# Routing of the third batch spread over more slots of the attention, and the experts' tile tables made in four pieces

## The chip, the core and the metric

The kernel runs on one core of a Trainium2 chip. Five engines work beside each other, each in the order of its own program: TensorE (PE in the profile; its weight loads are PEld), VectorE (DVE), ScalarE (ACT), GpSimd (POOL), and SyncE (SP), which issues most of the DMAs. They meet at semaphores. The metric is the time of one execution on the device in microseconds (us). The median of three runs before the change is 1767.79 us (1761.07 to 1770.71).

## The reference

Four blocks follow each other, each on the sum of what came before it and its own input normalised. x has the shape (4, 512, 256), that is 4 batches of 512 tokens. All is float32.

```python
x = x + linear_attention(layernorm(x))       # layer 0
x = x + hadamard_ffn(layernorm(x))
x = x + grouped_attention(layernorm(x))      # layer 1
x = x + attention_and_experts(layernorm(x))  # the block that is changed
```

The last block, with 32 query heads, 8 key heads, 16 experts and 4 experts to a token:

```python
h = rms(x, ln_w)
q, k = rope(h @ wq, h @ wk); v = h @ wv
scores = where(causal, q @ k.T / 8, -1e30)
x = x + (softmax(scores) @ v) @ wo
h = rms(x, ff_ln_w)
logits = h @ wg                              # (token, 16)
topv, topi = top_k(logits, 4)
weights = zeros.at[topi].set(softmax(topv))
a = silu(h @ w1[e]) * (h @ w3[e])            # for every expert e
moe = sum over e of weights[:, e] * (a @ w2[e])
out = x + moe
```

The kernel computes each token for its four experts alone.

## The kernel before

**Attention.** Each batch has four pairs of key heads, so there are 16 pairs, u = 0 to 15 (NU). A pair's scores are made in five fills f = 0 to 4, and one loop counts them as n = 5u + f, from 0 to 79, with four more turns, 80 to 83, in which only what is left of pair 15 is done. A turn does, in this order on each engine's program:

- fill (line 1287): PE makes the scores sc, in four PSUM banks.
- weighed (1408): DVE multiplies the products po of the pair before with the inverse sums (rsb) into oT; turn_blocks (1333): DVE transposes the last fill's exps into pT.
- inverses (1398): PE transposes the widened inverse sums into pq; out_proj (1421): PE multiplies oT with wo into py; q_lo and q_hi (1209, 1215): PE makes the next queries (pr), for ACT to copy (raw) and POOL to rotate (qr).
- least (1306): DVE masks the scores and takes their minima mx, which frees the banks sc.
- A string of signs for ACT (line 1888): a digit is the exps of one bank (exps, 1323), a "w" the widening of an inverse sum (widen, 1391), and a "." one copy out of PSUM that was put off (drain_one), if there is one.
- weigh (1354): PE makes the products po of exps and values, in parts: "3" at the end of fill 4 of the same pair (224 matmuls in the records), "02" in fill 0 and "1" in fill 1 of the next pair (168 and 104).

Everything on PE but the scores shares four further PSUM banks in turn (unit, line 1120). po takes all four. The copy y of py is added to z by POOL (line 1434).

**Routing.** When a batch's attention is done, each token's experts are chosen. route (line 1439) returns this work as a list of pieces: squares, mean, root, scale, rows_out, residual, turn_half, turned_both, logits, ranks (two, each with earlier and count), gates, shares, places, choose, and 16 scatters. A scatter is an indirect DMA of POOL that writes 128 tokens' rows to their place in the table xs in DRAM. Pieces are plain (False), use a PSUM bank (True), are scatters (None), or a pause, behind which only scatters follow in that slot. extras (line 1770) takes as many pieces as it is told. Every turn ends in a slot: extras with 1 to 3 plain pieces, up to 1 with a bank (only in fills 2 and 3) and 2 or 4 scatters (line 1901). In fill 1 of the odd pairs there is another slot in the middle, for one piece with a bank (line 1883).

Batch 2's routing (the third batch) is put in the list in fill 64, and its pieces run to the end of turn 82. Behind its choose comes plan_tiles(0).

**The tables of tiles.** The experts work in 79 tiles of 128 rows (NSLOT). A tile's expert, its first row and its row count come from the counts of rows by expert. plan_tiles (line 1662) makes a table of them in some 40 small DVE instructions; SP writes it to DRAM (list) and reads it back for all partitions (tall, lines 1746 and 1748). read_plan (1753) turns it into integers. There are two tables: phase 0, after batch 2, lays out 33 tiles (NFIRST), which hold rows of the first three batches only; phase 1, after batch 3, lays out the other 46.

**Experts.** Behind the attention a loop of steps n works on the tiles (lines 2037 to 2056): fetch_weights loads an expert's weights into wall, which takes the space of the attention's buffers; fetch_rows loads a tile's rows (xin), three steps ahead; turn_in transposes them (ptx, hTx); hidden makes ph, gx and ax; turn_hidden transposes (pa, aTx); give multiplies (pyx), weighs (yx) and adds to the result by an indirect DMA of POOL. Each step ends with two pieces of batch 3's routing, the list `pieces` (1918): 34 of them in steps 0 to 16, then plan_tiles(1), five empty ones, and read_plan(1).

Of the kernel before, what the change touches and what calls it, by code (L numbers as in the profile page):

```python
# [16 lines left out]
P = 128  # L17
# [9 lines left out]
NEXP = 16  # L27
# [62 lines left out]
def kernel(  # L90
# [64 lines left out]
    def C(name):  # L155
        cols = C_COLS[name]
        if cols.start < C_L0:
            return c_l0[0][:, cols]
        return cst[:, cols.start - C_L0 : cols.stop - C_L0]
# [782 lines left out]
    with ExitStack() as a1:  # L942
# [109 lines left out]
        for k in range(4 * NT * B + 2):  # L1052
            b, i = divmod(k, 4 * NT)
# [55 lines left out]
    with ExitStack() as a2:  # L1109
# [28 lines left out]
        def drain_one():  # L1138
            if held:
                held.pop(0)()  # L1140
# [521 lines left out]
        def plan_tiles(phase):  # L1662

            lo, hi = PHASES[phase]
            pos = C("iota")

            def small(name, n=NEXP):
                return rp.tile([P, n], F32, tag=name, name=name)

            cnt, tiles, first = small("cnt"), small("tiles"), small("first")  # L1670
            nc.vector.tensor_scalar(cnt, C("e16"), -float(CAP), 1.0, ALU.mult, ALU.add)
            nc.vector.tensor_tensor(cnt, cnt, run, ALU.add)

            cube = rp.tile([P, NEXP, NEXP], F32, tag="cube", name="cube")
            wide = [P, NEXP, NEXP]
            some = cnt
            if phase == 0:
                some = small("some")
                nc.vector.tensor_scalar(some, cnt, 0.5 - P, None, ALU.add)
            nc.vector.tensor_tensor(  # L1680
                cube, some.unsqueeze(2).to_broadcast(wide),
                C("m128").unsqueeze(1).to_broadcast(wide), ALU.is_gt,
            )
            nc.vector.tensor_reduce(tiles, cube, AX.X, ALU.add)
            nc.vector.tensor_tensor(tiles, tiles, taken, ALU.subtract)
            nc.vector.tensor_tensor(
                cube, C("before").rearrange("p (e f) -> p e f", f=NEXP),
                tiles.unsqueeze(1).to_broadcast(wide), ALU.mult,
            )
            nc.vector.tensor_reduce(first, cube, AX.X, ALU.add)  # L1690
            mine, past = small("mine"), small("past")
            nc.vector.tensor_scalar(mine, first, pos, None, ALU.is_le)
            nc.vector.tensor_tensor(past, first, tiles, ALU.add)
            nc.vector.tensor_scalar(past, past, pos, None, ALU.is_gt)
            nc.vector.tensor_tensor(mine, mine, past, ALU.mult)


            if phase == 0:


                nc.vector.tensor_scalar(
                    taken, first, -1.0, float(hi - lo), ALU.mult, ALU.add
                )
                nc.vector.tensor_scalar(taken, taken, 0.0, None, ALU.max)
                nc.vector.tensor_tensor(taken, taken, tiles, ALU.min)
                used, ahead, all_ = small("used"), small("ahead"), small("all", 1)
                nc.vector.tensor_scalar(used, taken, 0.0, None, ALU.is_gt)
                nc.vector.tensor_reduce(all_, used, AX.X, ALU.add)
                nc.vector.tensor_tensor(
                    cube, C("before").rearrange("p (e f) -> p e f", f=NEXP),  # L1710
                    used.unsqueeze(1).to_broadcast(wide), ALU.mult,
                )
                nc.vector.tensor_reduce(ahead, cube, AX.X, ALU.add)

                nc.vector.tensor_tensor(place, C("e16"), ahead, ALU.subtract)
                nc.vector.tensor_scalar(place, place, all_, None, ALU.add)
                nc.vector.tensor_tensor(ahead, ahead, place, ALU.subtract)
                nc.vector.tensor_tensor(ahead, ahead, used, ALU.mult)
                nc.vector.tensor_tensor(place, place, ahead, ALU.add)
            info = rp.tile([P, 5, NEXP], F32, tag="info", name="info")  # L1720
            off = small("off")
            if phase == 0:
                nc.vector.tensor_scalar(off, first, -1.0, None, ALU.mult)
            else:
                nc.vector.tensor_tensor(off, taken, first, ALU.subtract)
            nc.vector.tensor_scalar(off, off, float(P), None, ALU.mult)
            nc.vector.tensor_copy(info[:, 0, :], C("e16"))
            nc.vector.tensor_scalar(info[:, 1, :], C("e16"), float(CAP), None, ALU.mult)
            nc.vector.tensor_tensor(info[:, 1, :], info[:, 1, :], off, ALU.add)
            nc.vector.tensor_tensor(info[:, 2, :], cnt, off, ALU.subtract)  # L1730
            nc.vector.tensor_scalar(info[:, 3, :], place, float(WIDE), None, ALU.mult)
            nc.vector.tensor_tensor(
                info[:, :4, :], info[:, :4, :],
                mine.unsqueeze(1).to_broadcast([P, 4, NEXP]), ALU.mult,
            )
            nc.vector.scalar_tensor_tensor(
                info[:, 4, :], place, pos, C("e16"), ALU.is_equal, ALU.mult
            )
            tab = small("tab", 5)
            nc.vector.memset(tab, 0.0)  # L1740
            nc.vector.tensor_reduce(tab[:, :5], info, AX.X, ALU.add)
            at128 = small("at128", 1)
            nc.vector.tensor_scalar(at128, pos, float(P), None, ALU.mult)
            nc.vector.tensor_tensor(tab[:, 1:2], tab[:, 1:2], at128, ALU.add)
            nc.vector.tensor_tensor(tab[:, 2:3], tab[:, 2:3], at128, ALU.subtract)
            nc.sync.dma_start(out=lists[phase], in_=tab)

            nc.sync.dma_start(
                out=tall[:, lo:hi, :],
                in_=lists[phase][: hi - lo, :].unsqueeze(0).to_broadcast([P, hi - lo, 5]),  # L1750
            )

        def read_plan(phase):

            lo, hi = PHASES[phase]
            nc.vector.tensor_copy(starts[:, lo:hi], tall[:, lo:hi, 1])
            nc.vector.tensor_scalar(
                valid[:, lo:hi], tall[:, lo:hi, 2], C("iota"), None, ALU.is_gt
            )
            nc.vector.tensor_copy(wats[:, lo:hi], tall[:, lo:hi, 3])  # L1760
            if phase == 0:
                nc.vector.tensor_scalar(
                    wrows, tall[:, :NEXP, 4], float(P), None, ALU.mult
                )
# [3 lines left out]
        soon, later, thin, routed = [], [], [], []  # L1768
# [45 lines left out]
        for n in range(5 * NU + 4):  # L1814
            u, f = divmod(n, 5)
# [11 lines left out]
            if u % 4 == 0 and f == 4 and 0 < u < 4 * B:  # L1827
                later.extend(route(u // 4 - 1))
                if u // 4 == B - 1:
                    later.append((False, lambda: plan_tiles(0)))  # L1830
                    later.append(("pause", lambda: None))
                    later.append((False, lambda: read_plan(0)))

# [34 lines left out]
            if on:  # L1868
                if f == 1:
                    q_lo(2 * u + 2)  # L1870
                if f == 2:
                    q_hi(2 * u + 2)
                if f == 3:
                    q_lo(2 * u + 3)
                if f == 4:
                    inverses(u, 3)
                    q_hi(2 * u + 3)
                if keys_on and u % 2 == 0 and f in (1, 3):
                    keys_lo(q) if f == 1 else keys_hi(q)
                if keys_on and u % 2 == 1 and f in (2, 3):  # L1880
                    values(q, f - 2)
                least(n)
                if f == 1 and u % 2 == 1:
                    extras(0, 1)


                wide = {0: [(v, 1)] if v >= 0 else [], 3: [(u, 3)], 4: [(u, 0), (u, 2)]}
                for i in ("..w0123", "..0.1.23", ".0.12.3", "w.0.12.3", ".ww.0123")[f]:
                    if i == "w":
                        if wide[f]:  # L1890
                            widen(*wide[f].pop(0))
                    elif i == ".":
                        drain_one()
                    else:
                        exps(n, int(i))
            elif f == 0 and v >= 0:
                widen(v, 1)
# [20 lines left out]
        pieces = [piece for kind, piece in route(B - 1) if kind != "pause"]  # L1918
        pieces.pop(0)()

        pieces += [lambda: plan_tiles(1)] + 5 * [lambda: None] + [lambda: read_plan(1)]
        a2.close()
        w4.close()
        m1.enter_context(tc.manual_schedule())
# [329 lines left out]
```

## Time and profile before

| | before |
|---|---|
| median of three runs | 1767.79 us |
| profiled execution, its own time | 1779.78 us |
| its span, first to last instruction | 1777.9 us |
| mean granted PE clock | 0.966 |
| busy share PE, PEld, DVE, ACT, POOL | 91%, 53%, 56%, 46%, 50% |
| PE's share of the chain that ended last | 41% |
| DMA queue for instructions (q8) | 131 packets, 2.15 MB |
| plan_tiles(0) on DVE | 1422.10 to 1430.72 us |
| plan_tiles(1) on DVE | 1544.55 to 1550.03 us |
| batch 2's scatters on POOL | 1419.46 to 1455.76 us |

The profile is of one execution; it lasted 12 us longer than the median. A line of the timeline gives the start, the duration, the engine, the line of the code, the operation, the tile written and those read, the shapes, the number of instructions merged, and in brackets the idle time of the engine before them with what ended it; "issue" stands for a wait that no semaphore explains. A line of the stretches gives from:to, the length, and then for PE, PEld, DVE, ACT and POOL the busy time and the instructions, then the granted PE clock, the share of the DMA engines that was busy, and GB/s.

### The profile page before, as it was taken

The page shows a single profiled execution, that of the slowest core. Times are in us where ns is not written, and L with a number is a line of the kernel's source. Part 1 is how long each engine was busy: PE and PEld are TensorE (multiplying, and loading weights), DVE is VectorE, ACT ScalarE, POOL GpSimd, SP SyncE. Part 2 cuts the span into 40 slices and gives each one's busy share as a digit, 9 for nine tenths or more (in the row PEclk, how much of TensorE's full clock was granted, in tenths as well). Part 3 has the DMA queues.
Part 4 walks back from the last instruction along what each step waited for, and adds up shares of the span by engine and source line. Part 5 has one row for each costly group of instructions (what it writes and reads, how often), then busy time and mean ns, then how long its engine had stood idle before and what let it go on. Part 6 is the DMA issues. An engine that isn't in the chain of part 4 may idle for free.

```text
span 1777.9 us, 42123 instructions
## 1 busy us (share of the span) xinstructions
PE 1624.5 (91%) x16100; PEld 950.4 (53%) x16100; DVE 1002.4 (56%) x3069; ACT 825.5 (46%) x2162; POOL 894.5 (50%) x914
## 2 busy tenths in 40 slices
PE   7999999999999986899999999999989868899993
PEld 4665554553334223466666666666666635455552
DVE  4547336556666412667766686668756924433333
ACT  4431122125655762566666665666556514233331
POOL 3224133225565545755466647794667244844442
PEclk9999999999999997899999999999999979899997
DMA  9992000020000001322222222322222037655556
GB/s 348 371 369 84 0 1 0 1 102 1 1 1 1 1 1 43 77 55 56 56 56 55 56 56 56 87 75 59 61 61 68 6 122 235 154 97 87 86 88 167
DMA packets 106934, 146.59 MB, mean 82 GB/s; under 512 B 11632, under 2 KB 86128, under 8 KB 106352
## 3 DMA queue, kind: packets, MB, share of 16 engines
q1 hardware_dynamic: 91856, 123.54, 22.9%
q0 software_dynamic: 14448, 19.80, 6.5%
q8 instruction: 131, 2.15, 0.5%
q14 instruction: 67, 0.55, 0.1%
q10 hardware_dynamic: 432, 0.55, 0.1%
HBM read 67.17 MB, written 68.29 MB: 76 GB/s over the span
## 4 chain that ended last, share of the span: by engine, by line
PE 41%; POOL 5%; issue 5%; ACT 5%; DVE 4%; DMA 1%; SPq 0%; another core or an unknown queue 0%; ACTq 0%; DVEq 0%; POOLq 0%
PE po L1375 9%; PE ph L1947 8%; PE sc L1298 6%; PE py L1425 5%; PE pr L225 4%; PE pyx L1947 3%; ACT masked L1328 2%; PE pq L1403 1%; POOL xs L1612 1%; POOL part L1199 1%; DVE masked L1316 1%; ACT raw L1190 1%; PE ptx L1983 1%; PE pa L2016 1%; POOL qr L1200 1%
## 5 line engine op out<-in xcount | busy, mean ns | idle before, releaser
L1328 ACT ACTIVATE masked<-masked,mx 128x256 f32<-128x256 f32 (+3 forms) x512 | 281.1, 553 | 4.8 <-DVE mx L1316 4.8
L1316 DVE CUSTOM_DVE_ANT_0 masked<-sc,cst 128x256 f32<-128x256 f32 (+3 forms) x512 | 214.0, 481 | 44.6 <-PE sc L1298 44.5
L1375 PE MATMUL po<-pT,vsr 32*64 32x128 f32 (+1 forms) x8064 | 198.1, 289 | 39.6 <-issue 24.9
L1375 PEld LDWEIGHTS po<-pT,vsr 32*64 32x64 f32 x8064 | 158.3, 132 | 90.0 <-issue 41.8
L1345 DVE STREAM_TRANSPOSE pT<-masked 128x512 f32<-128x512 f32 x256 | 168.5, 691 | 57.7 <-ACT masked L1328 57.2
L2029 POOL DMA_INDIRECT acc<-yx,goes x79 | 123.2, 1559 | 138.9 <-ACT yx L2028 101.4
L335 DVE TENSOR_REDUCE top<-sc 128x1 f32<-128x512 f32 x256 | 158.7, 682 | 56.3 <-PE sc L329 56.3
L1298 PE MATMUL sc<-kr,qr 32*128 32x128 f32 (+3 forms) x2048 | 173.9, 460 | 10.8 <-POOL qr L1200 3.7
L1947 PE MATMUL ph<-wall,hTx 128*128 x316 | 163.5, 641 | 11.6 <-DVE hTx L1985 6.9
L995 ACT ACTIVATE pT<-sT 128x512 f32<-128x512 f32 x256 | 131.5, 604 | 60.8 <-PE sT L989 60.6
L1434 POOL TENSOR_TENSOR z<-z,y 128x256 f32<-128x256 f32 x64 | 47.3, 740 | 195.9 <-ACT y L1433 195.8
L1415 DVE TENSOR_TENSOR oT<-po,rsb 128x128 f32<-128x128 f32 x256 | 61.3, 287 | 139.4 <-PE po L1375 127.1
L2009 DVE TENSOR_TENSOR ax<-ph,gx 128x256 f32<-128x256 f32 x79 | 33.6, 425 | 166.2 <-ACT gx L2007 154.7
L1425 PE MATMUL py<-wo,oT 128*128 128x256 f32 x512 | 123.7, 390 | 2.3 <-DVE oT L1415 1.6
L1199 POOL TENSOR_TENSOR part<-raw,rtab 128x512 f32<-128x512 f32 x80 | 102.5, 1281 | 43.1 <-ACT raw L1190 39.8
L1298 PEld LDWEIGHTS sc<-kr,qr 32*128 32x128 f32 x2048 | 90.5, 189 | 60.5 <-issue 29.0
L225 PE MATMUL pr<-hT,wq 128*128 128x512 f32 x256 | 122.0, 601 | 0.0
L225 PE MATMUL pgu<-xnT,wug 128*128 128x512 f32 x256 | 114.5, 598 | 1.5 <-DVE xnT L190 1.5
L989 PE MATMUL sT<-qr,km 32*128 32x512 f32 x512 | 108.1, 634 | 7.0 <-POOL km L967 2.8
L1425 PEld LDWEIGHTS py<-wo,oT 128*128 128x128 f32 x512 | 94.6, 192 | 31.2 <-DVE pT L1345 7.6
L1406 ACT COPY rsb<-pq 128x512 f32<-128x512 f32 x64 | 36.0, 587 | 134.8 <-PE pq L1403 129.7
L1947 PEld LDWEIGHTS ph<-wall,hTx 128*128 128x128 f32 x316 | 55.8, 196 | 79.1 <-issue 43.2
(301 smaller groups left out, 2884.9 us busy)
## 6 DMA issues: line engine op xcount, KB each, us to landing
xs<-zero SPq DMA_DIRECT2D x16, 2304.0 KB
vsr<-vd SPq DMA_DIRECT2D x256, 64.0 KB
wall<-in_w_exp_dram SPq DMA_DIRECT2D x16, 768.0 KB
xin<-xs SPq DMA_DIRECT2D x79, 144.0 KB
wq<-in_w_q_dram SPq DMA_DIRECT2D x33, 256.0 KB
kr<-krq SPq DMA_DIRECT2D x32, 256.0 KB
acc<-zero SPq DMA_DIRECT2D x2, 2176.0 KB
vd<-vs SPq DMA_DIRECT2D x64, 64.0 KB
```

The source lines that it names most:

```text
L225: nc.tensor.matmul(dst, lhsT=w[:, c, cols], rhs=srcT[:, c, tok], start=(c == 0), stop=(c == n - 1),)
L335: nc.vector.tensor_reduce(top[:, at : at + 1], sc, AX.X, ALU.max)
L995: nc.scalar.activation(pT[:, g, :], us[g], AF.Exp)
L1199: nc.gpsimd.tensor_tensor(part, raw, R(name), ALU.mult)
L1298: nc.tensor.matmul(scs[s][:, at : at + w], lhsT=qrs[2 * u + jj][rows(s), ab, tok(t)], rhs=krs[u][rows(s), ab, :w], start=(ab == 0), stop=( ...
L1316: nc.vector.tensor_tensor_reduce(masked[:, part], sc[:, part], C("cmask")[:, S - (t + 1) * P :], 1.0, 3e38, ALU.add, ALU.min, mx[:, t, i : ...
L1328: nc.scalar.activation(part, part, AF.Exp, bias=lots[u, "mx"][:, t, i : i + 1], scale=-1.0, accum_out=lots[u, "sm"][:, t, i : i + 1],)
L1345: nc.vector.transpose(dst[:, 2 * (f % 2) + s // 2, :], p)
L1375: nc.tensor.matmul(heaps[u, phase][a][64 * g : 64 * g + 64, first * P : last * P], lhsT=vsrs[u][rows(a), c, 64 * g : 64 * g + 64], rhs=src ...
L1425: nc.tensor.matmul(py[:, :D], lhsT=oT[:, j, :], rhs=wo4[:, 4 * (u % 4) + j, :], start=(j == 0), stop=(j == 3),)
L1947: ins = nc.tensor.matmul(out, lhsT=lhsT, rhs=wall[:, bass.ds(w_at[i] + at, n)], **kw)
L2029: nc.gpsimd.indirect_dma_start(out=accs[i % 2][:, :], out_offset=bass.IndirectOffsetOnAxis(ap=goes[:, i : i + 1], axis=0), in_=y[:, :], in ...
```

## The change

Four edits:

1. extras(0, 1), the middle slot for one piece with a bank, is also called in fills 0 and 4 of pairs 13, 14 and 15 (u > 12). Before, these pairs had it in fill 1 only, and only where u is odd.
2. The strings for ACT get one more "." ahead of the widening in fills 0 and 4, for the copy of such a piece. In fill 4, in every pair, the copy raw of q_hi, which stood between the wides and the exps, now stands ahead of both wides.
3. plan_tiles becomes a generator with three yields, so that a table is made in four pieces: the count of tiles, the first tile of each expert, the masks (in phase 0 also the experts' places), the table itself with its DMAs. The first table's four pieces follow choose in the list as plain pieces.
4. The second table's four pieces take the place of the one, with four empty pieces behind them instead of five.

No instruction is added or removed but by the order.

```diff
@@ plan_tiles @@
             pos = C("iota")
+            wide = [P, NEXP, NEXP]
...
             nc.vector.tensor_reduce(tiles, cube, AX.X, ALU.add)
             nc.vector.tensor_tensor(tiles, tiles, taken, ALU.subtract)
+            yield
             nc.vector.tensor_tensor(
                 cube, C("before").rearrange("p (e f) -> p e f", f=NEXP),
                 tiles.unsqueeze(1).to_broadcast(wide), ALU.mult,
             )
             nc.vector.tensor_reduce(first, cube, AX.X, ALU.add)
+            yield
             mine, past = small("mine"), small("past")
...
                 nc.vector.tensor_tensor(place, place, ahead, ALU.add)
+            yield
             info = rp.tile([P, 5, NEXP], F32, tag="info", name="info")
@@ the loop of fills @@
                 later.extend(route(u // 4 - 1))
                 if u // 4 == B - 1:
-                    later.append((False, lambda: plan_tiles(0)))
+                    plan = plan_tiles(0)
+                    later.extend(4 * [(False, lambda: next(plan, None))])
                     later.append(("pause", lambda: None))
                     later.append((False, lambda: read_plan(0)))
...
                 least(n)
-                if f == 1 and u % 2 == 1:
+                if f == 1 and u % 2 == 1 or f in (0, 4) and u > 12:
                     extras(0, 1)
...
-                for i in ("..w0123", "..0.1.23", ".0.12.3", "w.0.12.3", ".ww.0123")[f]:
+                for i in ("...w0123", "..0.1.23", ".0.12.3", "w.0.12.3", "..ww.0123")[f]:
@@ ahead of the experts @@
-        pieces += [lambda: plan_tiles(1)] + 5 * [lambda: None] + [lambda: read_plan(1)]
+        plan2 = plan_tiles(1)
+        pieces += 4 * [lambda: next(plan2, None)] + 4 * [lambda: None]
+        pieces += [lambda: read_plan(1)]
```

More of the change, by code (lines that the diff above doesn't have):

```diff
@@ L1674, in plan_tiles @@
             cube = rp.tile([P, NEXP, NEXP], F32, tag="cube", name="cube")
-            wide = [P, NEXP, NEXP]
             some = cnt
```

## The prediction

> **What bounds the kernel now.** The share of busy time comes first (PE 91%, no other engine over 56%), then the 40 slices, where PE falls to 6 tenths around 1450 us, then stretches of 2.5 us there. Fill n is fill f = n mod 5 of pair u = n div 5. By the exps on ACT the last fill, 79, ends at 1420 us and the first expert's matmul starts at 1462.7; between them lies the drain of pair 15 that the change touches.
>
> ```profile
> 1417.00:1419.50 2.50, 2.22 (x103) 2.01 (x89) 2.40 (x13) 2.50 (x11) 0.04 (x1) 1.00 0.03 7
> 1422.00:1424.50 2.50, 1.59 (x17) 0.62 (x10) 2.26 (x10) 0.62 (x1) 2.15 (x4) 1.00 0.31 118
> 1424.50:1427.00 2.50, 1.00 (x4) 0.37 (x4) 2.26 (x11) 0.00 (x0) 2.15 (x4) 0.96 0.30 118
> 1427.00:1429.50 2.50, 2.05 (x4) 0.28 (x2) 2.22 (x13) 0.00 (x0) 2.15 (x4) 0.50 0.32 119
> 1434.50:1437.00 2.50, 1.82 (x10) 1.48 (x7) 1.77 (x10) 0.37 (x1) 0.00 (x0) 0.50 0.16 27
> ```
>
> The columns are PE, its weight loads, DVE, ACT, POOL, the granted clock, the DMA share and GB/s. In 7.5 us PE finishes 25 matmuls, while DVE (making the first table) and POOL (scatters) are full; then the clock is halved.
>
> ```profile
> 1383.09 4.50 PE L1375 MATMUL po<-pT,vsr 32*64 32x256 f32 x168
> ...
> 1420.01 2.71 PE L1375 MATMUL po<-pT,vsr 32*64 32x256 f32 x50
> 1423.02 0.46 PE L1375 MATMUL po<-pT,vsr 32*64 32x128 f32 x4 [0.30 <-issue]
> 1426.67 0.55 PE L1375 MATMUL po<-pT,vsr 32*64 32x256 f32 x1 [1.01 <-issue]
> 1430.94 3.85 PE L1375 MATMUL po<-pT,vsr 32*64 32x128 f32 x103 [0.95 <-issue]
> ```
>
> The timeline of PE: the 168 matmuls of a pair's part "02" take 4.50 us in pair 14 and 14.8 in pair 15 (1420.01 to 1434.79), with gaps in which PE waits for nothing that the profile shows. POOL scatters from 1419.46 to 1429.35. Of the 23 gaps of over 0.25 us from 1100 to 1456, 18 lie beside a scatter, nearly all in long runs of short matmuls. Four scatters at 1345.5, beside wider matmuls, caused none.
>
> ```profile
> 1450.11 0.72 POOL L1434 TENSOR_TENSOR z<-z,y 128x256 f32<-128x256 f32 x1 [1.08 <-ACT y L1433]
> 1450.99 0.98 POOL L1612 DMA_INDIRECT xs<-hx,ati  x1 [0.15 <-issue]
> 1455.81 0.73 POOL L1434 TENSOR_TENSOR z<-z,y 128x256 f32<-128x256 f32 x1
> ...
> 1456.57 0.37 SPq L1941 DMA_DIRECT2D wall<-in_w_exp_dram  x1
> ```
>
> The timelines of POOL and SP: y was copied by 1451.75, but its addition stands behind four scatters and ends at 1456.54. The first experts' weights, which take the space of the attention's buffers, are fetched right behind it.
>
> **The change part by part.** Following the lists through the slots, batch 2's routing moves so: turned_both from the end of fill 72 to the middle of 69, logits 73 to 70, ranks 75 and 76 to 71 and 72, gates 77 to 73, shares 78 to 74, places 78 to 75, choose 79 to 75, the 16 scatters from 79-82 to 75-78 (four each), the table from 80 to 76 (three pieces) and 77 (one), its reading from 81 to 78. Nothing is removed.
>
> The drain without them. Part "02": 14.8 - 4.5 = 10.3 us. The 4 transposes and 8 py behind it, at the halved clock: 1.09 + 3.62 against 0.66 + 1.99, 2.1. Part "1": 4.8 (1439.90 to 1444.70) against 2.51 in pair 14: 2.3. The last 24 py: 6.3 against 5.7, 0.6. The last addition: 4.8 from the end of y, against 0.73: 4.1. Together 19.4 us. DVE's table (1422.10 to 1430.72) lies beside part "02" and is in these terms. If the clock stays half, about 11 remain; that is the lower bound.
>
> Pair 15 pays, because DVE carries its fills (9.9 of 10 us busy from 1380 to 1410). Fill 75: two ranks' worth, 3.4, is replaced by choose, 1.9; but places puts 32 matmuls (3.1, 1408.62 to 1411.74) ahead of part "02", and ACT's copy of them makes ACT wait: DVE's next products come 2.1 later. Fill 76: 3.4 out, 6.5 in (1422.10 to 1428.61): +3.1. Fill 77: gates 0.5 out, 2.1 in: +1.6. Fill 78: shares against the reading, +0.2; the list takes 5.3 from its issue (1430.96) to the reading (1436.22), about as long as fill 78's minima are away, and behind the list's two DMAs on SP nothing is queued until the experts. Fill 79 loses choose: -1.8. Sum +5.2 on the chain.
>
> Pairs 13 and 14: PE's work is only moved. In fill 69 the copy out of turned_both stands behind the wides: 1.14 + 0.82 before part "3" has its fourth bank; in fill 70 the exps wait for the logits' copy. The ranks fall into DVE's waits (2.59 in fill 71, 1.96 in fill 72), 3.4 each. They ran 1.34 and 1.65 instead of 0.69 beside POOL's rope products at 1230.86. I take 2.0 in all; bounds 0 and 5.
>
> Scatters in pair 15: a group of four costs nothing (1345.5) or 4.8 us (1287.44 to 1292.23, where part "02" took 9.3, its halved clock included). Group 1 meets the last half of part "02" of fill 75: I take 1.5. Group 2 meets part "1", but DVE is at the table then. Group 3 meets wide matmuls. Group 4 meets the first half of part "3" in fill 79: 3.0. Together 4.5; bounds 0 and 9.6. POOL's additions z behind them wait up to 5 us, and need to be done only by the end.
>
> The clock in pair 15: PE waits some 2.5 us twice for DVE in fills 77 and 78, as long as the stretch at 1424.50. I take 1.0. The Trainium skill ("TensorE: Matmul & The Clock Gate", Part 1: The HAM clock gate) has the clock halved after an idle window of about 3.4 us and restored after a busy one. The rows agree, with 0.50 from 1427 to 1440; by that rule waits under 3.4 us would cost nothing, and the sum would be 1.0 better.
>
> The order in fill 4 of every pair: raw is now copied ahead of the two wides. It waits for pr anyway (0.18 us idle before it at 1001.92), so the eight exps end 1.14 later, 1007.5 instead of 1006.4. The transposes that read them start at 1008.36, behind products that wait for PE: nothing. Without that cover it is 1.14 x 16.
>
> The second table. Now DVE is held from 1544.55 to 1550.03, ph comes 3.3 us late, and SP, waiting for the table at its list, fetches the next rows at 1552.61:
>
> ```profile
> 1550.75 3.78 PE L1947 MATMUL ph<-wall,hTx 128*128 x4 [2.38 <-DVE tab L1745]
> 1556.65 0.69 PE L1983 MATMUL ptx<-ident,xin 128*128 128x128 f32 x2 [2.12 <-DMA xin<-xs]
> ```
>
> In four pieces it is 2.4 us beside step 17 and 3.0 beside step 18. The first hides in DVE's idle 2 us of a step, the second delays by 1.0. But the fetch behind the list stays late: rows land 6.7 us after the table's end as now, one step (3.25 us) further on, with the end 1.25 later. Gain 2.0, less 0.5 for a clock that halves in that wait: 1.5 (bounds 0 and 5.5, the whole hold). The reading comes one step later, at step 21; rows of the second table are fetched at step 30.
>
> Sum: -19.4 + 5.2 + 2.0 + 4.5 + 1.0 - 1.5 = -8.2 us. The profiled execution took 1779.78 (span 1777.9), 12.0 above the median of 1767.79; from it 1771.6 follows, from the median 1759.6.
>
> **The rivals.** All back (chance 0.20): the scatters miss the short matmuls, pairs 13 and 14 hide their part, the second table gives 3.0. -19.4 + 5.2 - 3.0 = -17.2, 1751 us. For it: 10 of 16 scatters of batch 1 caused no gap; against it: group 4 is timed on part "3". The Trainium skill ("Runtime: NRT & Kernel Launch", Instruction fetch mechanics) calls the refill of the instruction memory in 16 KiB blocks mostly hidden. The instruction queue's 131 packets and 2.15 MB fit such blocks, the gaps beside scatters don't fit the hiding; by the page the 4.5 would fall away.
>
> The gaps go along (0.20): groups 1 and 4 cost 4.8 each and the clock 3 in pair 15: -19.4 + 5.2 + 2.0 + 9.6 + 3.0 - 1.5 = -1.1, 1767. The change then only shifts the stall.
>
> The halved clock (0.12), the one that ends slower: the table in fill 76 leaves PE without work until fill 78, the clock drops there and, with PE waiting between parts, stays down to the end of the drain. 21 us of PE work (part "3" 4.5, the drain 16.5) at 3.62/1.99 become 17.2 longer: -8.2 - 1.0 + 17.2 = +8.0, 1776. It decides if the clock is below full when part "3" of pair 15 starts and hasn't returned within part "02". Against it: from 1440 on it returned after 9 us of work with gaps.
>
> **How the numbers follow.** My forecast, part of the drain comes back, has 0.48; its own range is 1754 to 1766. The time given is its 1760. The range reaches over "all back" to 1749 and over "the gaps go along" to 1772, leaving out the halved clock and the ends: about 0.8. 0.5% is 8.8 us, about what a measurement of this kernel can tell from no change. The forecast lies just at it: 0.22 of its 0.48 and 0.20 of "all back" are faster (0.42); slower is most of the halved clock (0.09); the rest 0.49.
>
> **What would show it.** Right: part "02" of pair 15 in 4.5 to 5 us at clock 1.0, the last z under 1.5 us behind its py, the wall's first fetch some 7 us earlier than 1456.57; DVE's fill 76 at about 12 us; gaps beside scatters in part "3" of pair 15. In the experts, one wait on xin behind the list and no wait on tab over 1 us. Wrong: gaps in the drain without scatters (then scatters weren't their cause), fills of pairs 0 to 12 longer (the fill-4 order), or pair 15 longer by more than 15 us.

## The result, and the profile after

The changed kernel took 1758.94 us (median of 22 runs, 1752.42 to 1764.40) against 1767.12 us (22 runs, 1759.02 to 1775.29) on the same chip: a ratio of 0.9955, 95% interval 0.9943 to 0.9967, or 8.2 us less. The forecast was 1760 us and a sum of -8.2 us. The total agrees. The experiments below do not confirm the split behind it. On two other chips the term put at zero is worth some 9 us by itself, and the moved routing, which was to carry most of the gain, costs time. On the chip of the result the parts never ran alone, and how they share the 8.2 us stays open.

The profiled execution after took 1758.13 us (span 1756.3) and is one of the 22. The span before was 1777.9, so the two traces differ by 21.6 us, 13 more than the medians. The execution profiled before (1779.78) is none of the 22 of its kernel, and slower than all of them. The record doesn't name its chip, and the experiments give reason to think that it was another one. What is read from this one pair of traces holds for these two executions first.

The stretches of the trace after, where the drain of pair 15 now is, and where DVE makes the first table (columns as before: PE, weight loads, DVE, ACT, POOL, clock, DMA share, GB/s):

```profile
1397.50:1400.00 2.50, 0.00 (x0) 0.00 (x0) 2.23 (x11) 0.00 (x0) 0.35 (x2) 0.71 0.16 59
1400.00:1402.50 2.50, 2.43 (x6) 1.99 (x7) 2.50 (x8) 0.00 (x0) 0.00 (x0) 0.50 0.00 0
1422.50:1425.00 2.50, 2.50 (x103) 2.13 (x105) 1.19 (x5) 0.79 (x2) 0.00 (x0) 1.00 0.03 7
1425.00:1427.50 2.50, 1.83 (x79) 1.61 (x64) 1.75 (x8) 0.00 (x0) 0.00 (x0) 1.00 0.02 7
```

PE is full in part "02" at clock 1.00, where it finished a few matmuls in a stretch before. The place in which PE has nothing to do has moved to fill 76, where the clock falls to 0.50. PE's timeline of the trace after:

```profile
1382.06 5.28 PE L1375 MATMUL po<-pT,vsr 32*64 32x256 f32 x168
...
1400.07 6.32 PE L1425 MATMUL py<-wo,oT 128*128 128x256 f32 x16 [4.06 <-DVE oT L1415]
...
1416.59 4.06 PE L1375 MATMUL po<-pT,vsr 32*64 32x128 f32 x220 [0.28 <-ACT rsb L1406]
...
1421.60 4.84 PE L1375 MATMUL po<-pT,vsr 32*64 32x256 f32 x168
1427.11 0.63 PE L1403 MATMUL pq<-ident,wide 128*128 128x128 f32 x4 [0.67 <-DVE oT L1415]
1427.57 1.89 PE L1425 MATMUL py<-wo,oT 128*128 128x256 f32 x8
1429.40 2.57 PE L1375 MATMUL po<-pT,vsr 32*64 32x128 f32 x104
1431.89 5.45 PE L1425 MATMUL py<-wo,oT 128*128 128x256 f32 x24
...
1537.61 0.44 PE L1989 MATMUL ptx<-ident,xin 128*128 128x128 f32 x2 [4.28 <-DMA xin<-xs]
```

Line by line: part "02" of fill 75 stands beside the first group of four scatters and takes 0.8 more than 4.50. In fill 76 PE waits 4.06 for DVE's products, which stand behind the table (1393.24 to 1399.80), and the next 16 py run at half the clock, 6.32 against 3.72. Part "3", beside the last group of scatters, loses 0.33. Then the whole drain runs without a gap: 4.84 where it was 14.8, 1.89 where it was 3.62, 2.57 where it was 4.8. The last line is the only wait of the experts on the second table's rows.

The end of the drain, POOL's and SP's timelines after:

```profile
1437.88 0.72 POOL L1434 TENSOR_TENSOR z<-z,y 128x256 f32<-128x256 f32 x1 [1.00 <-ACT y L1433]
```

```profile
1438.63 0.37 SPq L1947 DMA_DIRECT2D wall<-in_w_exp_dram  x1
1439.78 0.35 SPq L1965 DMA_DIRECT2D xin<-xs  x1
```

The last addition no longer stands behind scatters, and the weights' fetch is issued 17.9 us earlier than before's 1456.57; some 7 were forecast. Of the other 11, 8.5 are there already at the first minima of fill 69, ahead of nearly all that the change moves: they are the difference of the two executions.

### The profile page after: what moved, and what is told of

Its sections match the earlier page's. It is cut to its first block, busy times and chain, and to the rows that moved or that the text cites. A ratio compares the mean times of both kernels' runs of the same rounds, so it can differ in the third digit from the quotient of the medians.

```text
span 1756.3 us, 42143 instructions
## 1 busy us (share of the span) xinstructions
PE 1619.6 (92%) x16100; PEld 951.8 (54%) x16100; DVE 1005.8 (57%) x3069; ACT 824.8 (47%) x2162; POOL 896.2 (51%) x914
## 4 chain that ended last, share of the span: by engine, by line
PE 46%; DVE 4%; POOL 4%; issue 3%; ACT 2%; DMA 1%; SPq 0%; ACTq 0%; DVEq 0%; POOLq 0%
PE po L1375 9%; PE ph L1953 8%; PE sc L1298 8%; PE pr L225 6%; PE py L1425 5%; PE pyx L1953 3%; PE pq L1403 2%; PE pv L234 1%; PE ptx L1989 1%; PE pa L2022 1%; DVE masked L1316 1%; ACT raw L1190 1%; POOL part L1199 1%; POOL qr L1193 1%; DMA sum<-acc 1%
## 5 line engine op out<-in xcount | busy, mean ns | idle before, releaser
L1316 DVE CUSTOM_DVE_ANT_0 masked<-sc,cst 128x256 f32<-128x256 f32 (+3 forms) x512 | 213.8, 480 | 48.4 <-PE sc L1298 48.3
L1375 PE MATMUL po<-pT,vsr 32*64 32x128 f32 (+1 forms) x8064 | 187.6, 289 | 26.9 <-issue 12.3
L1298 PE MATMUL sc<-kr,qr 32*128 32x128 f32 (+3 forms) x2048 | 180.2, 470 | 11.9 <-POOL qr L1200 7.0
L1298 PEld LDWEIGHTS sc<-kr,qr 32*128 32x128 f32 x2048 | 93.4, 193 | 64.7 <-issue 28.2
L1425 PEld LDWEIGHTS py<-wo,oT 128*128 128x128 f32 x512 | 96.5, 196 | 34.6 <-DVE pT L1345 7.1
L1328 ACT ACTIVATION_READ_ACCUMULATOR masked<-masked,mx 128x1 f32 x512 | 97.4, 190 | 0.0
```

Of the source, the lines that this page charges most:

```text
L1298: nc.tensor.matmul(scs[s][:, at : at + w], lhsT=qrs[2 * u + jj][rows(s), ab, tok(t)], rhs=krs[u][rows(s), ab, :w], start=(ab == 0), stop=( ...
L1316: nc.vector.tensor_tensor_reduce(masked[:, part], sc[:, part], C("cmask")[:, S - (t + 1) * P :], 1.0, 3e38, ALU.add, ALU.min, mx[:, t, i : ...
L1328: nc.scalar.activation(part, part, AF.Exp, bias=lots[u, "mx"][:, t, i : i + 1], scale=-1.0, accum_out=lots[u, "sm"][:, t, i : i + 1],)
L1375: nc.tensor.matmul(heaps[u, phase][a][64 * g : 64 * g + 64, first * P : last * P], lhsT=vsrs[u][rows(a), c, 64 * g : 64 * g + 64], rhs=src ...
L1425: nc.tensor.matmul(py[:, :D], lhsT=oT[:, j, :], rhs=wo4[:, 4 * (u % 4) + j, :], start=(j == 0), stop=(j == 3),)
```

## The experiments

Twelve runs were made in three groups, each on one chip of its own beside the kernel before. That kernel took 1793.80 us in the first group (labels x_string, x_table2, x_route, x_latescat), 1768.01 in the second (x_after, x_behind, x_drain, x_pool) and 1787.15 in the third (y_). The chip of the second group is called the first chip here, and the result is counted with it: the medians (1767.12 and 1768.01) and the traces after agree. The chips of the first and the third group are called the second and the third chip. To compare traces, the time between fixed places is used: the first minima (L1316) of fills 65, 69, 75 and 79, and ph, the first expert's matmul. All in us, from the profiled execution of each kernel:

| kernel | chip | 65 to 69 | 69 to 75 | 75 to 79 | 79 to ph | ph to end |
|---|---|---|---|---|---|---|
| before | not recorded | 40.8 | 54.9 | 30.8 | 48.7 | 315.2 |
| after | first | 36.6 | 59.1 | 37.7 | 28.0 | 311.7 |
| x_after | first | 36.7 | 58.8 | 37.0 | 28.2 | 311.0 |
| x_behind | first | 37.0 | 53.3 | 32.2 | 56.9 | 313.5 |
| x_drain | first | 36.9 | 58.8 | 32.4 | 32.1 | 311.9 |
| x_pool | first | 37.2 | 60.5 | 39.9 | 29.4 | 314.3 |
| x_string | second | 44.2 | 58.2 | 30.9 | 46.3 | 315.0 |
| y_string | third | 43.8 | 53.6 | 32.5 | 46.2 | 315.5 |
| x_table2 | second | 44.3 | 64.0 | 34.6 | 50.4 | 312.7 |
| y_table2 | third | 43.5 | 58.7 | 32.5 | 45.5 | 315.1 |
| x_route | second | 40.8 | 65.2 | 49.7 | 30.0 | 315.5 |
| y_route | third | 43.4 | 68.9 | 41.9 | 32.6 | 315.8 |
| y_after | third | 43.1 | 67.7 | 43.0 | 29.8 | 312.6 |
| x_latescat | second | 43.8 | 66.6 | 43.0 | 42.3 | 314.0 |

The trace before doesn't look like one of the first chip. Fill 65, which is the same in the kernel before and in x_behind, takes 13.7 us in the trace before and 8.0 to 8.4 in all five traces of the first chip, but 13.4 to 14.5 in all eight of the other two. Its part "02", beside scatters of batch 1, takes 9.3 in the trace before, 4.6 to 4.8 on the first chip, and 8.6 to 10.9 on the others.

**The scatters out of the drain, nothing else (x_behind).** In the kernel before, batch 2's scatters wait until the loop of fills is over; the first table stays in the drain.

```diff
-                4 if u > 13 else 2,
+                0 if n > 78 else 4 if u > 13 else 2,
```

> The kernel before with batch 2's 16 scatters behind turn 83 instead of in turns 79 to 82; the rows' fetch then waits for them, so the total gets longer by about 12 us (16 x 1.26 less the 4.1 that stood in front of the last z, less what the drain gains). Only the drain tells. If the scatters cause its gaps: part "02" of pair 15 in 4.5 to 5 us, the clock at 1.0, the last z within 1.5 us of its py, and from pair 15's first products oT to the last z some 21 to 24 us instead of 38, bounded by DVE's table. If the table or something else causes them: part "02" over 8 us again.

1778.54 us, ratio 1.0065 (1.0040 to 1.0090): slower by 10.5. PE's drain in this trace:

```profile
1411.54 3.96 PE L1375 MATMUL po<-pT,vsr 32*64 32x256 f32 x149
1416.23 0.88 PE L1375 MATMUL po<-pT,vsr 32*64 32x128 f32 x19 [0.73 <-issue]
1422.75 1.09 PE L1403 MATMUL pq<-ident,wide 128*128 128x128 f32 x4 [5.64 <-DVE oT L1415]
1423.63 3.62 PE L1425 MATMUL py<-wo,oT 128*128 128x256 f32 x8
1427.18 2.90 PE L1375 MATMUL po<-pT,vsr 32*64 32x128 f32 x104
1430.02 5.45 PE L1425 MATMUL py<-wo,oT 128*128 128x256 f32 x24
1460.82 0.66 PE L1983 MATMUL ptx<-ident,xin 128*128 128x128 f32 x2 [25.36 <-DMA xin<-xs]
```

Part "02" takes 5.6 us from its start to its end (11.54 to 17.11) where it took 14.8 in the trace before. From pair 15's first products oT to the end of the last addition it is 26.9 us, against 38.0 in the trace before and 18.7 in the one after; 21 to 24 at full clock were expected. DVE's table, which the long part "02" had covered, now shows by itself: as the wait of 5.64 and as half the clock in the 8 py. So, by these three traces, some 11 us of the drain's gain belong to the scatters and some 8 to the table. But this trace is of the first chip, where scatters beside such matmuls cost next to nothing in fill 65, and the trace before is probably not; that the scatters cause the gaps is shown by the other two chips (x_latescat, below). The scatters, now from 1437 to some 1457, hold up the rows xin instead, which are read from the table xs that they write.

**The first table back in the drain (x_drain).** The changed kernel, with the table's pieces in turns 80, 80, 81 and 82 and the reading behind them.

```diff
-                    later.extend(4 * [(False, lambda: next(plan, None))])
-                    later.append(("pause", lambda: None))
-                    later.append((False, lambda: read_plan(0)))
+                    table = {80: 2, 81: 1, 82: 1}
...
+            for _ in range(table.get(n, 0)):
+                next(plan, None)
...
+        read_plan(0)
```

> The changed kernel with the first table's pieces moved from fills 76 and 77 into DVE's waits of the drain: two pieces at the end of turn 80, one each in 81 and 82, the reading behind the drain. DVE carries pair 15's fills, so fills 76 and 77 should get shorter by 5 to 6 us (8.6 out, PE's own work then bounds); the drain pays 0.5 for the third piece and the experts' weights wait some 2 us for the reading. Sum -3.5 against the changed kernel. If the clock, which halved in fill 77, stays full as well, -5. The rival, that pair 15 is bound elsewhere (the scatters' gaps), expects 0 to +2.

1759.72 us, 0.9949 (0.9927 to 0.9970), the same as the changed kernel in this group (x_after, next), where -3.5 us was expected. The columns show both sides: 75 to 79 is 4.6 shorter, 79 to ph 3.9 longer. Between these two places it makes no difference where the table's pieces stand: in the drain without scatters they cost about what they cost in fills 76 and 77.

**The changed kernel again (x_after).** No edit.

> The changed kernel once more, beside the kernel before on the chip of this call, as the control for the others. The prediction's sum expects -8 us. On the chip of the runs before, the change without the second table's pieces was 4 us slower than the kernel before, with gaps beside the scatters in fills 75 and 76; if that is a matter of the chip (how far the scatters hold up the instructions there), the changed kernel shows the same gaps and -8 to +4; if it was a matter of that kernel, it shows none and -8 to -12.

1760.01 us, 0.9949 (0.9931 to 0.9967). It repeats the result, in the time and in every column of the trace.

**The second table's DMAs from POOL (x_pool).** The changed kernel, list and tall of the second table issued by POOL.

```diff
-            nc.sync.dma_start(out=lists[phase], in_=tab)
+            by = nc.gpsimd if phase else nc.sync
+            by.dma_start(out=lists[phase], in_=tab)
...
-            nc.sync.dma_start(
+            by.dma_start(
```

> The changed kernel with the two DMAs of the second table issued by POOL instead of SP, so that the rows' fetch on SP isn't queued behind them. The wait of 4.28 us of ptx on xin should go: -4 us against the changed kernel, if POOL's additions, which then stand behind the list, have their 4 us of slack (four yx buffers of 3.25 us a step). The rival, that ACT's yx waits for POOL then, expects -1 to +2.

1764.57 us, 0.9984 (0.9965 to 1.0002): 4.6 slower than x_after, instead of 4 faster; neither the sum nor the rival (-1 to +2) expected it. The wait on xin is gone, and a longer one has taken its place. POOL's and then PE's timeline:

```profile
1546.79 1.21 POOL L1750 DMA_DIRECT2D list<-tab  x1
1551.03 0.61 POOL L1752 DMA_DIRECT2D tall<-list  x1 [3.03 <-DMA list<-tab]
```

```profile
1555.46 2.07 PE L1954 MATMUL ph<-wall,hTx 128*128 x2 [4.37 <-DVE hTx L1992]
```

On SP the second DMA is issued 1.4 us behind the first (1530.65 and 1532.07 in the trace after); on POOL 4.24 behind, with the results' scatters queued in between. The table lands later, DVE waits 7.41 for it at the reading, and with it PE.

**The order in fill 4 alone (x_string, y_string).**

```diff
-                for i in ("..w0123", "..0.1.23", ".0.12.3", "w.0.12.3", ".ww.0123")[f]:
+                for i in ("..w0123", "..0.1.23", ".0.12.3", "w.0.12.3", "..ww.0123")[f]:
```

> The kernel before with one sign moved: in fill 4 of all pairs raw is copied ahead of the two wides. The prediction's step (the exps end 1.14 us later, under the cover of part "3") expects no change, -1 to +2 us. The rival, that this order is on the path, expects up to 1.14 us in each of 16 pairs, +5 to +18 us. Its profile is also a second look at the drain of the kernel before: if the scatters cause the gaps there, part "02" of pair 15 again takes well over 4.5 us (8 to 15) with gaps beside scatters.

> The order of the string in fill 4 alone. If nothing waits for the wides, 0.999 to 1.001, and the 0.9944 of the first run was that chip's. If raw, copied earlier, lets POOL rotate and PE go on sooner in each of 16 pairs, 0.993 to 0.996 again, and the time from the first minima of pair 1 to those of fill 65 is shorter by 4 us or more than in the kernel before.

1784.47 us, 0.9944 (0.9914 to 0.9973), on the second chip and 1777.98 us, 0.9949 (0.9921 to 0.9976), on the third: faster by some 9 us both times, where nothing was expected. The gain isn't spread over the 16 pairs, which is what the rival expected. Part "02" of pair 15 takes 14.4 and 14.6 us with gaps beside the scatters, as was expected if these cause them.

Over all traces, four without this edit and ten with it, four fills before fill 65 are shorter by more than 0.5 us: fills 4 and 5 (8.58 to 7.26 and 9.64 to 8.92, means) and fills 34 and 35 (10.97 to 9.10 and 9.10 to 8.34). That is 4.7 us, on all chips alike. Fill 3, though, is longer (8.34 to 8.89), and the whole way from the first minima of fill 0 to those of fill 65 is 580.3 and 577.3 in the means, with single traces from 572.8 to 583.0. On the first chip alone it is 576.2 without the edit (x_behind) and 575.7 in the mean of four traces with it: there the sum doesn't show the 4.7. PE at fills 4 and 34, first in the kernel before, then in x_string:

```profile
740.78 3.73 PE L1375 MATMUL po<-pT,vsr 32*64 32x128 f32 x220 [1.55 <-ACT raw L1190]
744.43 1.12 PE L1298 MATMUL sc<-kr,qr 32*128 32x512 f32 x3
746.36 1.99 PE L1298 MATMUL sc<-kr,qr 32*128 32x512 f32 x13 [0.81 <-issue]
...
1006.32 1.80 PE L1375 MATMUL po<-pT,vsr 32*64 32x128 f32 x81 [1.48 <-issue]
```

```profile
746.20 3.73 PE L1375 MATMUL po<-pT,vsr 32*64 32x128 f32 x220 [0.38 <-ACT raw L1190]
749.85 2.81 PE L1298 MATMUL sc<-kr,qr 32*128 32x512 f32 x16
...
1008.72 3.84 PE L1375 MATMUL po<-pT,vsr 32*64 32x128 f32 x220 [0.38 <-ACT raw L1190]
```

In pair 0 part "3" needs the bank that the copy raw frees, and raw stood behind two wides (1.14 us): a true wait of 1.55 becomes 0.38. In pair 6 the wait on raw is the same, 0.38, in both; a gap of 1.48 that stands behind no semaphore is gone. The gap stands at the same matmul, 81 from the end of the part, in all four traces without the edit, and in none with it. Over the whole of fills 5 to 65 the means differ less, 540.2 and 537.8, with a spread of single traces of some 5 us. On the second and third chip 69 to 75 differs as well: 58.2 and 53.6 in x_string and y_string against 64.0 and 58.7 in x_table2 and y_table2, 5.5 in the mean of two and two. There, too, are gaps beside scatters, those of batch 1 in fills 69 and 70. The 4.7 and the 5.5 together come near to the measured 9, but they are stretches picked from single traces; why an edit of fill 4 should meet the scatters otherwise isn't shown.

**The second table alone (x_table2, y_table2).**

The kernel before, with plan_tiles in pieces as in the change, the first table's run through at once:

```diff
-                    later.append((False, lambda: plan_tiles(0)))
+                    later.append((False, lambda: list(plan_tiles(0))))
...
-        pieces += [lambda: plan_tiles(1)] + 5 * [lambda: None] + [lambda: read_plan(1)]
+        plan2 = plan_tiles(1)
+        pieces += 4 * [lambda: next(plan2, None)] + 4 * [lambda: None]
+        pieces += [lambda: read_plan(1)]
```

> The kernel before with the second table alone in four pieces. The prediction's step expects -1.5 us, bounds 0 and -5.5; the two traces side by side (315.2 against 311.7 us from the first expert's matmul to the end) expect up to -3.5. The wait on DVE's table in front of ph goes, the wait of ptx on xin behind the list stays at 2 to 4 us. The rival, that the hold on DVE is made up for elsewhere, expects 0.

> The second table alone in four pieces. By the trace of the changed kernel, where the time from the first expert's matmul to the end was 3.5 us shorter, 0.998 to 0.9985; by its first run 1.0004 to 1.0056. If the pieces help only behind the moved routing, the time from the first expert's matmul to the end is 315 us as before and the ratio 1.000.

1796.43 us, 1.0030 (1.0004 to 1.0056), on the second chip and 1783.71 us, 0.9970 (0.9942 to 0.9999), on the third. The two contradict each other beyond their intervals: either the edit does different things on the two chips, or such runs don't settle an effect of this size. The traces say a little more. From ph to the end the six traces with the old table take 315.1 us in the mean (313.5 to 315.8), the eight with four pieces 312.9, x_pool among them (311.0 to 315.1); y_table2 itself shows no gain there. A comparison in the third group goes the same way: y_after, which has this edit, took 4.5 us less than y_route, which has all the others.

**Routing and first table, without the second (x_route, y_route).** The changed kernel less its fourth edit:

```diff
-        plan2 = plan_tiles(1)
-        pieces += 4 * [lambda: next(plan2, None)] + 4 * [lambda: None]
+        pieces += [lambda: list(plan_tiles(1))] + 5 * [lambda: None]
         pieces += [lambda: read_plan(1)]
```

> The change without the second table's pieces: slots, strings and first table as in the changed kernel. The prediction expects what is left of the sum, -6.7 us (-8.2 without -1.5); the traces, which put 3.5 us into the second table, expect -4.7. If the second table is the whole of the gain, 0.

> The routing moved and the first table in pieces, without the second table's pieces. By my sum -4.7 to -6.7 us (0.996 to 0.9975), with under five gaps of over 0.25 us in PE's matmuls of pair 15. If the gaps go along, as in its first run (1.0021), over ten such gaps and a ratio of 1.000 to 1.003.

1797.61 us, 1.0021 (1.0001 to 1.0041), on the second chip and 1789.46 us, 1.0011 (0.9977 to 1.0044), on the third: not the gain of the sum, but what was expected if the gaps go along. These kernels hold the edit of fill 4, too: against x_string and y_string of the same groups the routing with the first table costs 13.1 and 11.5 us. The columns say where, in means of two traces each: 75 to 79 45.8 against 31.7, 69 to 75 67.0 against 55.9, and from 79 to ph 31.3 against 46.3. The drain gains 15.0 and the fills pay 25.2, which leaves 10.2 of the measured 11.5 to 13.1.

**All parts together on the third chip (y_after).** The changed kernel.

> The changed kernel beside its three parts on one chip. If the parts add up, its ratio to before is that of routing, string and second table taken together (0.9945 to 0.9960 where before takes some 1767 us); if the gaps beside the scatters follow the routing on this chip, as they did in the first run of the routing alone, it is 0.998 to 1.001 and part "02" of fill 75 or part "3" of fill 79 takes 8 us or more.

1784.98 us, 0.9984 (0.9951 to 1.0017): no gain that can be told from nothing. The parts, each from another comparison, give -9.2 (y_string), +11.5 (y_route over y_string) and -3.4 (y_table2), -1.1 in all, against -2.2 measured. Part "3" of fill 79 takes 8.2 us, as was expected if the gaps go along. PE's gaps in y_after beside scatters, of batch 1 in fill 70 (the scatters run from 1345.75 to 1350.55) and of batch 2 in fill 76 (1413.60 to 1418.39):

```profile
1347.61 3.03 PE L1375 MATMUL po<-pT,vsr 32*64 32x256 f32 x46
1351.41 4.40 PE L1375 MATMUL po<-pT,vsr 32*64 32x256 f32 x122 [0.77 <-issue]
...
1414.92 0.34 PE L1375 MATMUL po<-pT,vsr 32*64 32x128 f32 x2 [0.30 <-issue]
1415.65 0.45 PE L1375 MATMUL po<-pT,vsr 32*64 32x128 f32 x3 [0.39 <-issue]
1416.43 2.12 PE L1375 MATMUL po<-pT,vsr 32*64 32x128 f32 x9 [0.33 <-issue]
1419.27 0.70 PE L1375 MATMUL po<-pT,vsr 32*64 32x128 f32 x3 [0.72 <-issue]
```

Gaps of over 0.15 us that no semaphore explains, within 1 us of a scatter, are counted from 1000 us to ph: PE has 23 in this trace, 10.3 us in all, and 1 of 0.6 us in the trace of the same kernel after (3 with 1.3 in x_after). The trace before has 23 with 8.8. The first lines are of scatters that the change doesn't touch: part "02" of fill 70 now stands behind the logits (1.86 us of PE), which were moved ahead, and meets them. Fill 70 takes 14.26 in y_after, 7.25 in y_string.

**Scatters held back once more (x_latescat).** The changed kernel, with batch 2's scatters not before turn 79.

```diff
-                4 if u > 13 else 2,
+                (0 if 74 < n < 79 else 4) if u > 13 else 2,
```

> The changed kernel with batch 2's 16 scatters alone held back to turns 79 to 82, where they stood before; the routing and the table stay early. If the scatters cause the gaps of the drain (the prediction), part "02" of pair 15 takes 8 to 15 us again, the last additions stand behind scatters for 4 us, and the time is 10 to 19 us over the changed kernel, +2 to +11 over the kernel before. If DVE's table in the drain was the cause, only the 4 us of the last addition come back: -4 us against the kernel before, with no gaps.

1799.53 us, 1.0029 (0.9997 to 1.0062): no better and no worse than x_route's 1797.61 in the same group, from which it differs by these scatters and the second table's pieces. The changed kernel itself didn't run in this group, so the expected +10 to +19 us over it weren't tested. Eight scatters in a row, 1430.67 to 1440.6, met the scores of fill 79. DVE's and ACT's lines ("remote" stands for a release that this core's profile doesn't show):

```profile
1440.05 0.42 DVE L1316 CUSTOM_DVE_ANT_0 masked<-sc,cst 128x256 f32<-128x256 f32 x1 [4.00 <-remote]
```

```profile
1442.34 0.58 ACT L1406 COPY rsb<-pq 128x512 f32<-128x512 f32 x1 [7.92 <-remote]
```

PE's part "3" waited 5.40 us for that rsb in turn. The part "02" behind took its 4.50 without a gap, with no scatter beside it, where 8 to 15 were expected; the last addition again stood 4.1 us behind scatters, as expected. The next four scatters, 1458.7 to 1463.5, met part "1" and the last py. PE's timeline in x_latescat, then in x_route:

```profile
1457.22 2.53 PE L1375 MATMUL po<-pT,vsr 32*64 32x128 f32 x88
1460.04 0.47 PE L1375 MATMUL po<-pT,vsr 32*64 32x128 f32 x6 [0.29 <-issue]
1460.80 1.87 PE L1375 MATMUL po<-pT,vsr 32*64 32x128 f32 x10 [0.29 <-issue]
1463.02 7.77 PE L1425 MATMUL py<-wo,oT 128*128 128x256 f32 x24 [0.35 <-issue]
```

```profile
1458.91 2.56 PE L1375 MATMUL po<-pT,vsr 32*64 32x128 f32 x104
1461.41 5.45 PE L1425 MATMUL py<-wo,oT 128*128 128x256 f32 x24
```

Part "1" takes 5.8 us to the start of the py where it takes 2.5 without scatters, and 79 to ph takes 42.3 against 30.0. The first table is early in both kernels, so on this chip the stall comes with the scatters and not with the table. The other traces agree: on the second and third chip part "02" of pair 15 takes 14.4 to 15.1 us in the four traces with scatters beside it, and 4.5 to 4.7 in the four without. Moving scatters moves the stall, here also to other engines.

## Why the prediction was right in its sum and wrong in its split

Step by step, the forecast first, then what the runs showed.

- **The drain, -19.4.** Right in the pair of traces it was made for: the stretch from pair 15's first products oT to the end of the last addition went from 38.0 to 18.7, -19.3, with each piece as told (part "02" 4.84, the 8 py 1.89, part "1" 2.57, the last addition 0.72 behind its y). On the second and third chip it is 34.6 to 39.2 in the four traces with the old order and 18.3 to 18.5 in the three with the new, -17.8 in the means. On the first chip the old drain was never traced. An estimate: x_behind differs from the kernel before only behind turn 78, took 10.5 us (7.1 to 15.9) longer, and spent 56.9 from 79 to ph; that leaves 46.4 (41 to 50) for the kernel before, against 28.2 in x_after, so -18 (-13 to -22).
- **DVE in pair 15, +5.2.** Right in this pair of traces: fills 75 to 78 +2.2, +3.1, +1.8, -0.2, and -1.3 in fill 79, +5.6 in all, against the forecast's +2.1, +3.1, +1.6, +0.2, -1.8. The measured sum holds the scatters and the clock of the next two points. On the first chip, against x_behind, 75 to 79 is longer by 5.5 in the trace after and 4.8 in x_after.
- **Scatters in pair 15, +4.5.** Missed, on opposite sides. In the trace after, groups 1 and 4 show 0.8 and 0.3 in PE's lines, and nothing is left for them in the fills' sum. On the second and third chip 75 to 79 is 14.1 longer (x_route and y_route against x_string and y_string), some 7 more than the 6.9 from before to after: the rival in which the gaps go along.
- **The clock, +1.0.** The clock did fall in fill 76 and 16 py took 2.6 longer, but DVE was behind by more than that in the same fill, and its +3.1 came out as told. It was back at 1.00 for the drain, so the rival of the halved clock didn't decide. The prediction's "The rows agree" goes too far for the trace before: the longest wait of PE ahead of the fall at 1427 is 1.01 us.
- **Pairs 13 and 14, +2.0.** Too small: +4.2 from before to after (69 to 75, 54.9 to 59.1), and on the first chip +5.8 for after and +5.5 for x_after against x_behind's 53.3. Fills 71 and 72, which the ranks fell into, are 2.4 and 2.0 longer. The forecast had set their 3.4 each against DVE's waits of 2.6 and 2.0 and noted that they run slower beside POOL's products, but didn't add it up. The ranks' products took 1.65 there, against 0.69 with POOL idle in the trace before:

```profile
1344.66 1.65 DVE L1533 TENSOR_TENSOR both<-both,cst 128x512 f32<-128x512 f32 x1
1346.35 1.64 DVE L1536 TENSOR_TENSOR both<-both 128x512 f32<-128x512 f32 x1
```

  On the second and third chip it is 11.1, with fills 69 and 70 under batch 1's scatters; the forecast had put nothing for these in this term.
- **The order in fill 4, 0.** This is the step that failed on the two chips on which it ran alone: -9.3 and -9.2 us. "The transposes that read them start at 1008.36, behind products that wait for PE: nothing" was read at one pair, and only downstream of the exps. What waits for raw itself wasn't asked: PE does, in pair 0, for 1.55 us. And the pair that was read, pair 6, holds a gap of 1.48 that vanishes with the edit. These and their neighbours are the 4.7 us of four fills; where the rest comes from isn't shown, nor how much of it is left on the first chip.
- **The second table, -1.5.** Of this size: the one wait on xin behind the list came as told (4.28, at the rows of the second table), none on tab over 1 us, and the traces' stretch behind ph is 2.2 us shorter in the mean, 3.5 in the pair of before and after. The two runs on it alone disagree, so no better number is given. x_pool shows that POOL's queue is no way round the remaining wait.

For the first chip the split can be reckoned in two ways, and they contradict each other. Taking the means over all chips, the order has -3.7 (fill 4, and the means of fills 5 to 65) to -4.7 (its four fills) and the second table -2.2 to -3.5, which leaves 0 to -2.3 of the -8.2 for the moved routing with the first table. Taking the first chip alone, the drain's -18, the +5.5 of 69 to 75 and the +4.8 of 75 to 79 make -7.7 for it, near the -6.7 of the forecast, and leave next to nothing for the order and the second table. Each rests on single traces and medians that are uncertain by several us; the parts didn't run alone there, so the split stays open. Either way it is luck that the sum came out to 0.1 us: the scatters' 4.5 didn't come in the trace after, pairs 13 and 14 cost 2 to 4 more than forecast, and the second table brought about 1 or 2 more.

On the third chip all parts ran: the order -9.2, the routing with the first table +11.5, the second table -3.4, and together -2.2, not to be told from zero. That is nearest to the rival in which the gaps go along (-1.1), though not by its sum, which has no gain of the order in it.

PE has 19 to 32 gaps beside scatters in all eight traces of the second and third chip, and 1 to 3 in the five of the first. The trace before, with 23, would be an exception only if it was taken on the first chip. Why the chips, or their executions, differ so stays open: no run changed only that.

## What to carry to other kernels

A stall that comes from what runs beside it, not from a semaphore, can be moved by a reordering instead of removed: price it at its new place with the full size it had at the old one, and ask what other work the moved pieces push under stalls of the same kind. An edit to the order that repeats in every pair is to be read in every pair, for what waits on each moved instruction, the copies out of PSUM above all. Before two traces are subtracted, compare a stretch in which both run the same code: fill 65 at 13.7 us in the trace before and 8.35 in x_behind tells that these two don't belong together. And a sum that comes out doesn't confirm its terms; run the parts beside each other on one chip before believing the split.

## What the runs showed of the hardware

- The changed kernel had 1 gap of 0.6 us beside scatters in its trace on the first chip and 23 of 10.3 us on the third, where the kernel before took 19 us longer. The same fill 65 took 8.35 us in x_behind and 14.5 in y_table2.
- Apart from the scatters, PE stands still for 1.1 to 1.7 us at fixed places of its program. In the trace before, such gaps end at 789.37, 833.70, 918.37, 963.84, 1006.32, 1052.34 and 1100.02, and between them PE ran 762, 1397, 761, 634, 762 and 762 matmuls; x_behind and y_table2 have them at the same matmuls. With the order of fill 4 changed they shift by a few matmuls, and the one at 1006.32 is hidden. The Trainium skill ("Runtime: NRT & Kernel Launch", Instruction fetch mechanics) describes instructions that are fetched in blocks of 256, at a cost mostly hidden. Regular places in the program fit blocks, but 762 matmuls and as many weight loads are about six such blocks, and no run here shows that these gaps are fetches.
- Beside eight scatters in a row (x_latescat) ACT waited 7.92 us and DVE 4.00 us for nothing that the profile of this core shows.
- DVE's products of 128x512 took 1.65 us beside POOL's products of the same size (from 1344.19 in the trace after), and 0.69 with POOL idle (1386.90 in the trace before).
